# Moving a table copy behind the last adjacency chunk, and two short tiles behind that chunk's lists

## The chip, the core and the metric

The kernel runs on one core of one Trainium2 chip. The metric is the device time of one execution in microseconds (us). Three runs of the kernel before gave 941.17, 937.54 and 940.53 us, so the median is 940.53 us. A separate execution was recorded by the hardware profiler; the durations below come from that one.

## What is computed

The reference is a two-layer graph network on 3327 nodes with 512 features and one sparse adjacency matrix (each node also neighbours itself). Cut to what matters:

```python
# layer 0: graph attention, 4 heads of 128
feats  = einsum('nf,hfo->hno', x, W)
logits = leaky_relu(e_s[:, :, None] + e_n[:, None, :], 0.2) - 1e10 * (1 - A)
out0   = relu(einsum('hnm,hmo->hno', softmax(logits), feats) + b)   # heads side by side
x      = layernorm(x + out0)
# layer 1: gated sum of an attention and a plain neighbour sum
attn_a = sigmoid(concat([adj @ x, x]) @ Wa.T + ba)                  # attn_b likewise
e      = where(adj != 0, exp(-leaky_relu(s_left[:, None] + s_right[None, :], 0.01)), 0)
x_a    = (e / (sum(e) + 1e-5)) @ (x @ W_sa)
x_b    = adj @ (x @ W_gcnb) + b_gcnb
x      = layernorm(x + sigmoid(attn_a * x_a + attn_b * x_b))
```

## The kernel before

All of it is `sparse_pass`; a dense pass stands behind it for graphs that are too dense, and does not run here. Nodes are padded to 3328, that is 26 tiles of 128. The first 12 tiles form group 0, the other 14 form group 1. In each group the nodes are sorted by their number of neighbours, so that each tile has a fixed cap of neighbours (`CAPS`, line 26).

**First stage, lists and features.** The adjacency comes in seven column chunks of 512 (the last has 256). Each chunk is 13 loads of two row tiles (`load_adj`, line 218) into 12 buffers (`AT`, line 34), all issued by SyncE (SP) in program order. For every chunk, TensorE (PE) sums the ones into codes (`add_codes`, line 396), ScalarE (ACT) takes them out of PSUM (`take_codes`, line 413), PE transposes them (`turn_codes`, line 421), and VectorE (DVE) picks the neighbours of each node from them (`top_codes`, `decode`, `pick`). Alongside, `features` (line 365) computes one tile of projected features, and GpSimd (POOL) writes the rows to `table0` in HBM. When a group's chunks are done its lists are sorted by length (`rank_a`, `rank_b`; for group 0 also `sort0`). The lists of group 0 are complete before the last chunk comes; the ranks of group 1 need the last chunk.

**`table0`.** For each node of group 0 it has two rows side by side (`twos`): the node's own x, and its features. The x rows are copied from HBM to HBM by one DMA, `x_rows` (line 238), which SP issues before the 13 loads of the last chunk. For group 1 a second table, `own1`, is put together by two more copies (lines 989 and 990), which are the next DMAs on SP.

**Gathers.** Neighbours' rows are fetched by indirect DMAs, one for each list position of a tile (128 rows of 2080 bytes), all issued by POOL in order (`indirect`, line 615). A tile's first gather brings the pair of own x and own features. They go to a ring of 42 slots (`RING`, line 33). `plan` (line 620) lists every gather of a layer in `waiting`; `gather` (line 656) issues them as long as the ring has room; `free` gives a tile's slots back. `at_first` (line 874) takes the gathers of features of the first two tiles out of the list and issues them ahead of the two own pairs, since these alone need the copied x rows.

**Second stage, layer 0.** Tiles are taken in `order0` (line 735): first tiles 11 and 10 (caps 5 and 6, called `early`), then tile 0 (cap 14, with an extra row for nodes over the cap), tile 1, and so on. For each tile `weigh_a` and `weigh_b` (DVE, with an exponential on ACT) make the attention weights, `attend` (line 784) scales each gathered row (DVE, every third one ACT) and sums the rows on PE with an identity matrix in fp32, and `finish` (line 881) adds the result to own x. The two early tiles are handled inside the first stage: they are weighed before `add_codes` of the last chunk, attended right after it, and finished before its `turn_codes`. From tile 0 on, a loop over the 26 tiles (line 948) does the rest, followed by layer 1 (lines 1139 to 1199), which gathers from `table1`.

Each engine takes its instructions in program order; the order above is written by hand. The part of the last chunk reads:

Of the kernel before, what the change touches and what calls it, by code (L numbers as in the profile page):

```python
# [25 lines left out]
CAPS = (14, 12, 11, 10, 9, 9, 8, 8, 7, 6, 6, 5) + (14, 13, 11, 10, 10, 9, 9, 8, 8, 7, 7, 6, 5, 4)  # L26
# [6 lines left out]
RING = 42  # L33
# [45 lines left out]
def sparse_pass(  # L79
# [39 lines left out]
    nc = tc.nc  # L119
# [8 lines left out]
    chunks = list(range(0, NP, CH))  # L128
    T0 = (0, NG[0])
# [7 lines left out]
    N0 = NG[0] * P  # L137
    table0 = dram.tile([N0 + NP, ROW], F32, name="table0")
    twos, singles = table0[: 2 * N0, :], table0[2 * N0 :, :]
# [36 lines left out]
    def place(j):  # L176

        return (0, j) if j < NG[0] else (1, j - NG[0])
# [5 lines left out]
    def row1(j):  # L184
        g, i = place(j)
        return x1[g][:, i, :]

    def slots(j):

        return S + 1 if j in T0 else CAPS[j] + 1  # L190
# [18 lines left out]
    def load_x(i):  # L209
        if i < len(chunks):  # L210
            cw = min(CH, NP - chunks[i])
            xc = xcs[i] = pj.tile([P, KT, CH], F32, tag="xc", name=f"xc{i}", bufs=3)
            nc.sync.dma_start(xc[:, :, :cw], xB[i] if cw == CH else xL)
# [20 lines left out]
        asa_rows.append(a_row)  # L234
    load_x(1)
    for i in range(len(chunks)):
        if i == len(chunks) - 1:
            x_rows = nc.sync.dma_start(twos.rearrange("(n t) w -> n t w", t=2)[:, 0, :], xo[:N0]).ins
            tc.add_to_no_dep_group("x rows", x_rows)
        load_adj(i)  # L240
        load_x(i + 2)


    nc.vector.memset(ones, 1.0)
# [368 lines left out]
    waiting, ends_at = [], {}  # L613

    def indirect(out_, table, ap):
        return nc.gpsimd.indirect_dma_start(  # L616
            out=out_, out_offset=None, in_=table, in_offset=bass.IndirectOffsetOnAxis(ap=ap, axis=0)
        ).ins
# [37 lines left out]
    def gather():  # L656

        while waiting and waiting[0][0] - freed[0] <= RING:
            indirect(*waiting.pop(0)[1:])

    def free(j):

        freed[0] = ends_at[j]
# [71 lines left out]
    order0 = first[-2:][::-1] + first[:-2] + second[-3:-2]  # L735
# [8 lines left out]
    def weigh_a(j):  # L744
        c = slots(j)
        g, i = place(j)
        w = ws[j] = m0.tile([P, S + 1, H], F32, tag="w", name=f"w{j}", bufs=3)
        es = srt[g][:, i : i + 1, S + 2 : S + 2 + H].bitcast(F32)
        for s0, n, buf, o in got[j]:
            nc.vector.tensor_add(w[:, s0 : s0 + n, :], buf[:, o : o + n, F : F + H], es.to_broadcast([P, n, H]))  # L750
        if j in T0:
            logit = m0.tile([P, H], F32, tag="logit", name=f"logit{j}")
            nc.vector.tensor_add(logit, stair[j][:, F : F + H], es2[g])
            small = psx.tile([P, B * H], F32, tag="pcol", name=f"to_nodes{j}", bufs=2)
            nc.vector.tensor_tensor(
                w[:, C0 + 1 :, :], to_nodes(m0, small, f"n{j}", logit),
                no_step.rearrange("p (b o) -> p b o", o=1).to_broadcast([P, B, H]), ALU.add,
            )
        nc.vector.scalar_tensor_tensor(w[:, :c], w[:, :c], 0.2, w[:, :c], ALU.mult, ALU.max)
        mx = m0.tile([P, 1, H], F32, tag="mx", name=f"mx{j}")  # L760
        nc.vector.tensor_reduce(mx[:, 0, :], w[:, :c].rearrange("p s h -> p h s"), AX.X, ALU.max)
        nc.vector.tensor_sub(w[:, :c], w[:, :c], mx.to_broadcast([P, c, H]))  # L762
        nc.scalar.activation(w[:, :c], w[:, :c], AF.Exp)  # L763

        for s0, n, buf, o in got[j]:
            a = max(s0, 1)
            if a == s0 + n:
                continue
            nc.scalar.copy(srt[g][:, i, a : s0 + n], buf[:, o + a - s0 : o + n, F + H])
        if j in T0:  # L770
            nc.scalar.copy(ids2[g], stair[j][:, F + H : F + H + 1])
        nc.scalar.copy(row1(j)[:, 0:F], got[j][0][2][:, 0, 0:F])

    def weigh_b(j):
        c, w = slots(j), ws[j]
        den = m0.tile([P, 1, H], F32, tag="den", name=f"den{j}")
        nc.vector.tensor_reduce(den[:, 0, :], w[:, :c].rearrange("p s h -> p h s"), AX.X, ALU.add)
        nc.vector.reciprocal(den, den)
        nc.vector.tensor_mul(w[:, :c], w[:, :c], den.to_broadcast([P, c, H]))  # L779
        if j in T0:  # L780
            small = psx.tile([P, B * H], F32, tag="pcol", name=f"to_rows{j}", bufs=2)
            ws2[j] = to_rows(m0, small, f"n{j}", w[:, C0 + 1 :, :])

    def attend(j, lean, between):


        w = ws[j]
        acc = accs[j] = ps.tile([P, F], F32, tag="acc", name=f"acc{j}", bufs=2)
        if not lean:
            nc.tensor.matmul(acc, ident, bias0, start=True, stop=False)  # L790
        for s0, n, buf, o in got[j]:
            for s in range(s0, s0 + n):
                gv = buf[:, o + s - s0, 0:F].rearrange("p (h o) -> p h o", h=H)
                if s % 3 == 2:
                    for h in range(H):
                        nc.scalar.activation(gv[:, h, :], gv[:, h, :], AF.Copy, scale=w[:, s, h : h + 1])  # L796
                else:
                    nc.vector.tensor_tensor(  # L798
                        gv, gv, w[:, s, :].rearrange("p (h o) -> p h o", o=1).to_broadcast([P, H, FO]), ALU.mult
                    )  # L800
                row = buf[:, o + s - s0, 0:F]
                if lean and s == 0:
                    nc.vector.tensor_add(row, row, bias0)
                nc.tensor.matmul(  # L804
                    acc, ident, row, start=(lean and s == 0), stop=(s == CAPS[j] and j not in T0)
                )
                if s == 2:
                    between()
        if j in T0:
            gv = stair[j][:, 0:F].rearrange("p (h o) -> p h o", h=H)  # L810
            nc.vector.tensor_tensor(
                gv, gv, ws2[j].rearrange("p (h o) -> p h o", o=1).to_broadcast([P, H, FO]), ALU.mult
            )
            nc.tensor.matmul(acc, to_node, stair[j][:, 0:F], start=False, stop=True)
# [54 lines left out]
        ps = ctx.enter_context(tc.tile_pool(name="ps", bufs=1, space=PSUM))  # L869
        ring = gp.tile([P, RING, ROW], F32, name="ring")  # L870

    early = order0[:2]

    def at_first():

        a, b = (CAPS[j] + 1 for j in early)
        waiting[: a + b] = waiting[1:a] + waiting[a + 1 : a + b] + [waiting[0], waiting[a]]
        for _ in range(a + b - 2):
            tc.declare_no_dep(indirect(*waiting.pop(0)[1:]), group="x rows", reason="they read rows of features only")

    def finish(j):
        y = row1(j)[:, 0:F]
        nc.vector.scalar_tensor_tensor(y, accs[j], 0.0, y, ALU.max, ALU.add)
        free(j)
        gather()
# [5 lines left out]
    for i in range(len(chunks)):  # L891
        if i == len(chunks) - 1:
            open_pools()
            for j in order0:
                plan(table0, j)
            at_first()
            gather()
            for j in early:
                weigh_a(j)
                weigh_b(j)  # L900
        add_codes(i)
        if i == len(chunks) - 1:
            for j in early:
                attend(j, False, lambda: None)
        take_codes(i)
        if i == len(chunks) - 1:
            for j in early:
                finish(j)
        more(1)
        if i == NC0:  # L910
            rankis[0] = rank_b(0)
            sort0(rankis[0])
        turn_codes(i)
        if i == NC0 + 2:
            climb(0, p0, psl.tile([P, CH], F32, tag="pc1", name="climb0")[:, : B + H])
        top_codes(i)
        decode(i)
        pick(i)
        if i == NC0 - 1:
            rank_a(0)  # L920
        if i == NC0:
            with nc.allow_non_contiguous_dma(reason="a word of a row"):
                nc.scalar.dma_start(
                    twos.rearrange("(t p o) w -> p t o w", p=P, o=2)[:, :, 1, F + H : F + H + 1],
                    ranks[0][:, : NG[0]].rearrange("p (t w) -> p t w", w=1),
                )
        more(4)
        if i == 0:
            stairs_ready()
# [12 lines left out]
        nc.tensor.matmul(psum, ones, v1[:, k, :], start=(k == 0), stop=(k == KT - 1))  # L942
    nc.vector.tensor_copy(v1sum, psum)
    norm = Norm(m0, "n0", {3, 7, 11, 15, 19, 22, 24, 25})
    weigh_a(order0[2])
    weigh_b(order0[2])
    ready = [[], []]
    for i in range(NT + 3):
        for args in ready[0]:
# [9 lines left out]
        if 0 < i <= NT:  # L959
            j = order0[i - 1]  # L960
# [189 lines left out]
    for i in range(NT + 3):  # L1150
        j, j1, jp, jpp = at_(i), at_(i + 1), at_(i - 1), at_(i - 2)
# [500 lines left out]
```

## Time and profile before

| | us |
|---|---|
| median of 3 runs | 940.53 |
| span of the profiled execution | 1066.8 |
| time of that run | 1068.62 |
| busy PE, DVE, POOL, ACT in that span | 814.2, 735.3, 593.5, 289.0 |
| start to first row scaled for tile 0 on DVE | 270.8 |
| from there to the last row written to `table1` | 359 |
| from there to the end | 437 |

The profiled execution is 126 us longer than the median of the others, so its durations are somewhat long for an ordinary run. Busy shares are averages over stages with different limits. In the first 250 us the DMA engines are busy all the time; after that they are at 56 to 63 per cent. The granted TensorE clock was 0.865 of full speed on average; it falls to one half when PE has had little to do.

The page's table of DMA issues gives the sizes that matter here: 13 loads of 256 KB for the last chunk, 3120 KB for the copy of x rows, and 3640 KB for each of the two copies to `own1`.

### The profile page before, as it was taken

Reading aid. Unit: us, or ns where it says so; the run is one execution under the profiler, and the core shown is the slowest. Engines: PE = TensorE matmul, PEld = TensorE weight load, DVE = VectorE, ACT = ScalarE, POOL = GpSimd, SP = SyncE. Lnnn points to the kernel's source line nnn. Section 1 sums busy time; section 2 is a strip of 40 time slices with the busy share of each in tenths; the row PEclk is TensorE's granted clock in tenths of the full one; section 3 lists DMA queues with packets and bytes.
Section 4 is the critical chain, followed back from the end, with each engine's and each line's share of the span. In section 5 each row is a group of like instructions: output and inputs, shape, how many; then the busy total and the mean of one; then the engine's idle time right before and its main releaser. Section 6 shows DMA issues by size and latency. Waiting matters only on the chain. (4 is left out here: it accounts for less than half of the span.)

```text
span 1066.8 us, 10313 instructions
## 1 busy us (share of the span) xinstructions
PE 814.2 (76%) x2518; PEld 426.4 (40%) x2518; DVE 735.3 (69%) x2100; ACT 289.0 (27%) x820; POOL 593.5 (56%) x641
## 2 busy tenths in 40 slices
PE   5698972521987877777987956639999999969993
PEld 4476751201443433333443422214444444434441
DVE  3486788407857467655756757348798998989973
ACT  1122220200424243432434422112323123232331
POOL 7511243760566666465766247765667777757611
PEclk9898995565898879788987977769999999989997
DMA  9999899991477668586676127755656666746400
GB/s 341 371 361 399 342 325 351 377 386 53 126 212 235 199 192 251 144 307 197 183 210 198 61 98 196 207 164 140 188 144 186 183 182 182 195 129 182 167 28 35
DMA packets 73349, 224.68 MB, mean 211 GB/s; under 512 B 12736, under 2 KB 16784, under 8 KB 72384
## 3 DMA queue, kind: packets, MB, share of 16 engines
q0 software_dynamic: 46368, 153.69, 48.8%
q1 hardware_dynamic: 24256, 68.13, 16.8%
q10 hardware_dynamic: 2656, 2.10, 0.6%
q8 instruction: 23, 0.38, 0.1%
q14 instruction: 46, 0.38, 0.1%
HBM read 203.02 MB, written 31.51 MB: 220 GB/s over the span
## 5 line engine op out<-in xcount | busy, mean ns | idle before, releaser
L616 POOL DMA_INDIRECT ring<-table,srt x464 | 475.2, 1024 | 265.1 <-issue 98.8
L804 PE MATMUL acc<-ring,ident 128*128 128x512 f32 x504 | 261.9, 667 | 56.6 <-ACT ring L796 18.5
L1097 DVE SCALAR_TENSOR_TENSOR sw<-ring,e,sw 128x512 f32<-128x512 f32 x226 | 169.4, 750 | 11.6 <-ACT sw L1081 4.7
L804 PEld LDWEIGHTS acc<-ring,ident 128*128 128x128 f32 x504 | 101.7, 212 | 178.8 <-issue 109.2
L1118 PE MATMUL acc<-ring,ident 128*128 128x512 f32 x264 | 126.4, 613 | 13.8 <-DMA ring<-table,srt 9.7
L372 PE MATMUL pf<-w,xc 128*128 128x260 f32 x416 | 105.3, 417 | 13.1 <-DVE w L312 13.1
L798 DVE TENSOR_TENSOR ring<-ring,w 128x512 f32<-128x512 f32 x176 | 111.3, 691 | 1.7 <-DVE w L779 1.2
L1137 PE MATMUL po<-wsa,sT 128*128 128x512 f32 x208 | 98.4, 617 | 18.5 <-ACT sT L1130 10.3
L372 PEld LDWEIGHTS pf<-w,xc 128*128 128x128 f32 x416 | 85.8, 209 | 30.1 <-DVE w L312 13.8
L1137 PE MATMUL po<-wg,sT 128*128 128x512 f32 x208 | 93.8, 593 | 0.8 <-issue 0.8
L796 ACT ACTIVATE ring<-ring,w 128x128 f32<-128x128 f32 x304 | 91.5, 389 | 0.0
L1118 PEld LDWEIGHTS acc<-ring,ident 128*128 128x128 f32 x264 | 50.7, 194 | 81.8 <-issue 54.7
L1137 PEld LDWEIGHTS po<-wsa,sT 128*128 128x128 f32 x208 | 40.9, 199 | 73.4 <-issue 59.3
L1099 DVE TENSOR_TENSOR ring<-ring 128x512 f32<-128x512 f32 x94 | 65.0, 692 | 3.2
L403 PE MATMUL pc<-at,pow 128*32 128x512 bf16 (+1 forms) x182 | 24.6, 414 | 53.0 <-DMA at<-in_adjB 24.4
L384 POOL DMA_DIRECT2D table<-row x26 | 14.3, 549 | 87.2 <-ACT st L381 84.6
L763 ACT ACTIVATE w<-w 128x40 f32<-128x40 f32 (+10 forms) x26 | 6.2, 237 | 201.5 <-DVE w L762 124.8
L1137 PEld LDWEIGHTS po<-wg,sT 128*128 128x128 f32 x208 | 39.3, 190 | 49.9 <-issue 49.7
L1130 ACT COPY sT<-pt 128x512 f32<-128x512 f32 x52 | 28.7, 587 | 102.0 <-remote 48.8
L376 ACT COPY row<-pf 128x512 f32<-128x512 f32 x26 | 15.2, 585 | 96.2 <-PE pf L372 50.6
L829 ACT COPY xt<-x1t 128x512 f32<-128x512 f32 x26 | 15.2, 584 | 94.9 <-remote 39.2
L835 PEld LDWEIGHTS pcol<-v,xt 128*128 128x128 f32 x208 | 33.1, 228 | 17.3 <-issue 14.1
(254 smaller groups left out, 941.7 us busy)
## 6 DMA issues: line engine op xcount, KB each, us to landing
at<-in_adjB SPq DMA_DIRECT2D x78, 512.0 KB
ring<-table,srt POOLq DMA_INDIRECT x464
table<-row POOLq DMA_DIRECT2D x26, 260.0 KB
xc<-in_xB SPq DMA_DIRECT2D x6, 1024.0 KB
own<-in_xo SPq DMA_DIRECT2D x1, 3640.0 KB
own<-table SPq DMA_DIRECT2D x1, 3640.0 KB
at<-in_adjL SPq DMA_DIRECT2D x13, 256.0 KB
table<-in_xo SPq DMA_DIRECT2D x1, 3120.0 KB
```

The lines of the kernel that those rows point to most:

```text
L372: nc.tensor.matmul(pf[:, hh, :HC], xc[:, k, o : o + P], w0[:, k, hh, :], start=(k == 0), stop=(k == KT - 1))
L403: nc.tensor.matmul(pc[32 * c : 32 * c + 32, : nt * P], pow2[:, s, :], loaded[i, m], start=(s == 0), stop=(m + 1 not in ms or s == 3),)
L616: return nc.gpsimd.indirect_dma_start(out=out_, out_offset=None, in_=table, in_offset=bass.IndirectOffsetOnAxis(ap=ap, axis=0)).ins
L796: nc.scalar.activation(gv[:, h, :], gv[:, h, :], AF.Copy, scale=w[:, s, h : h + 1])
L798: nc.vector.tensor_tensor(gv, gv, w[:, s, :].rearrange("p (h o) -> p h o", o=1).to_broadcast([P, H, FO]), ALU.mult)
L804: nc.tensor.matmul(acc, ident, row, start=(lean and s == 0), stop=(s == CAPS[j] and j not in T0))
L835: nc.tensor.matmul(pcol, xt1[:, k, :], v1[:, k, :], start=(k == 0), stop=(k == KT - 1))
L1097: nc.vector.scalar_tensor_tensor(sw, g[:, i, 0:F], e[:, s : s + 1], sw, ALU.mult, ALU.add)
L1099: nc.vector.tensor_add(g[:, i, 0:F], g[:, i - 1, 0:F], g[:, i, 0:F])
L1118: nc.tensor.matmul(plain[j], to, row, start=(not sums_of_two and i == 0), stop=(sums_of_two and i == len(rows) - 1),)
L1130: nc.scalar.copy(sT, pt)
L1137: nc.tensor.matmul(proj[j], sT[:, k, :], wt[:, k, :], start=(half + k == 0), stop=(half + k == KT))
```

## The change

The copy of x rows is issued after all loads of the last chunk, and so just ahead of the copies to `own1`. `at_first` now covers three tiles: it issues the 26 gathers of features of tiles 11, 10 and 0 (5 + 1, 6 + 1 and 14 + 1 list positions and the extra row, less the three own pairs), and leaves the three own pairs at the head of what waits. The weighing, attending and finishing of tiles 11 and 10 move from around `add_codes` of the last chunk to behind the ranks of group 1; tile 0 is weighed between their `attend` and their `finish`.

```diff
     for i in range(len(chunks)):
-        if i == len(chunks) - 1:
-            x_rows = nc.sync.dma_start(twos.rearrange("(n t) w -> n t w", t=2)[:, 0, :], xo[:N0]).ins
-            tc.add_to_no_dep_group("x rows", x_rows)
         load_adj(i)
         load_x(i + 2)
+    x_rows = nc.sync.dma_start(twos.rearrange("(n t) w -> n t w", t=2)[:, 0, :], xo[:N0]).ins
+    tc.add_to_no_dep_group("x rows", x_rows)
...
-    early = order0[:2]
-
     def at_first():
 
-        a, b = (CAPS[j] + 1 for j in early)
-        waiting[: a + b] = waiting[1:a] + waiting[a + 1 : a + b] + [waiting[0], waiting[a]]
-        for _ in range(a + b - 2):
-            tc.declare_no_dep(indirect(*waiting.pop(0)[1:]), group="x rows", reason="they read rows of features only")
+        whole, part, owns = [], [], []
+        for j in order0[:3]:
+            n = CAPS[j] + 1 + (j in T0)
+            whole, part, owns = whole + waiting[:n], part + waiting[1:n], owns + waiting[:1]
+            del waiting[:n]
+        assert whole[-1][0] <= RING
+        waiting[:0] = owns
+        for args in part:
+            tc.declare_no_dep(indirect(*args[1:]), group="x rows", reason="they read rows of features only")
...
             at_first()
             gather()
-            for j in early:
-                weigh_a(j)
-                weigh_b(j)
         add_codes(i)
-        if i == len(chunks) - 1:
-            for j in early:
-                attend(j, False, lambda: None)
         take_codes(i)
-        if i == len(chunks) - 1:
-            for j in early:
-                finish(j)
         more(1)
...
     norm = Norm(m0, "n0", {3, 7, 11, 15, 19, 22, 24, 25})
+    for j in order0[:2]:
+        weigh_a(j)
+        weigh_b(j)
+    for j in order0[:2]:
+        attend(j, False, lambda: None)
     weigh_a(order0[2])
     weigh_b(order0[2])
+    for j in order0[:2]:
+        finish(j)
     ready = [[], []]
```

## The prediction

> **What bounds the kernel now.** First the windows: busy time by engine over the stretch in which the first stage ends (columns: stretch, its us, PE, PEld, DVE, ACT and POOL busy with counts, granted TensorE clock, DMA share, GB/s).
>
> ```profile
> 164.00:178.00 14.00, 4.36 (x16) 2.29 (x16) 12.19 (x55) 0.68 (x1) 10.45 (x11) 0.50 1.03 324
> 178.00:187.00 9.00, 0.40 (x2) 0.11 (x2) 8.14 (x39) 0.00 (x0) 0.44 (x1) 0.50 1.02 360
> ...
> 191.00:204.00 13.00, 3.42 (x17) 1.30 (x15) 8.77 (x26) 6.92 (x23) 9.95 (x11) 0.50 1.04 395
> 204.00:222.00 18.00, 15.37 (x34) 6.57 (x32) 0.00 (x0) 0.47 (x1) 13.25 (x14) 0.88 1.03 387
> 222.00:244.00 22.00, 0.00 (x0) 0.00 (x0) 1.40 (x3) 0.00 (x0) 12.29 (x13) 0.50 0.98 368
> 244.00:264.00 20.00, 4.52 (x12) 2.96 (x12) 16.54 (x70) 0.00 (x0) 0.00 (x0) 0.50 0.04 15
> 264.00:271.00 7.00, 3.01 (x9) 2.15 (x10) 4.89 (x18) 3.05 (x10) 0.95 (x1) 0.50 0.15 39
> ```
>
> Up to 244 the DMA engines are full; up to 191 DVE is nearly full too. From 204 to 244 DVE does 1.4 us of work in 40, and POOL then has none for 20. The whole chip waits for a chain, which the timelines give. SP first (start, duration):
>
> ```profile
> 156.87 0.56 SPq L238 DMA_DIRECT2D table<-in_xo  x1
> 157.52 32.45 SPq L222 DMA_DIRECT2D at<-in_adjL  x13
> 190.02 0.67 SPq L989 DMA_DIRECT2D own<-in_xo  x1
> ```
>
> The copy of x rows goes out at 156.9, all 13 loads of the last chunk after it. POOL:
>
> ```profile
> 164.35 1.00 POOL L616 DMA_INDIRECT ring<-table,srt  x1 [6.48 <-DMA at<-in_adjB]
> ...
> 186.56 0.94 POOL L616 DMA_INDIRECT ring<-table,srt  x1 [8.72 <-DMA table<-in_xo]
> ...
> 267.61 0.95 POOL L616 DMA_INDIRECT ring<-table,srt  x1 [24.72 <-ACT x1a L772]
> ```
>
> Eleven gathers of features start at 164.35, one each 1.25 us; the own pairs wait until 186.56 for the copy; at 267.61 POOL comes out of 24.7 us of idleness, because the ring is full of rows that tile 0 has yet to use. DVE:
>
> ```profile
> 193.89 0.18 DVE L750 TENSOR_TENSOR w<-ring,srt 128x24 f32<-128x24 f32 x1 [2.24 <-DMA at<-in_adjL]
> ...
> 197.49 5.63 DVE L798 TENSOR_TENSOR ring<-ring,w 128x512 f32<-128x512 f32 x9
> 229.22 0.69 DVE L883 SCALAR_TENSOR_TENSOR x1a<-acc,x1a 128x512 f32<-128x512 f32 x1 [26.09 <-remote]
> 240.57 0.69 DVE L883 SCALAR_TENSOR_TENSOR x1a<-acc,x1a 128x512 f32<-128x512 f32 x1 [10.66 <-remote]
> 243.98 0.40 DVE L71 MAX8 ent<-pv 128x8 f32<-128x224 f32 x1 [2.72 <-remote]
> ...
> 263.76 0.22 DVE L750 TENSOR_TENSOR w<-ring,srt 128x60 f32<-128x60 f32 x1 [0.23 <-issue]
> ...
> 270.81 0.68 DVE L798 TENSOR_TENSOR ring<-ring,w 128x512 f32<-128x512 f32 x1
> ```
>
> The early tiles are weighed at 193.9 and scaled by 203.1. Then DVE waits for PE: their sums come at 229.2 and 240.6, the lists of the last chunk only at 244.0, and tile 0 is weighed at 263.8 and attended from 270.8. PE:
>
> ```profile
> 203.24 2.07 PE L790 MATMUL acc<-bias,ident 128*128 128x512 f32 x2
> ...
> 212.65 6.17 PE L804 MATMUL acc<-ring,ident 128*128 128x512 f32 x14
> 218.66 0.47 PE L427 MATMUL pv<-ident,v 128*128 128x128 f32 x3
> ```
>
> PE's last adjacency matmul starts at 202.9; then come 15 fp32 matmuls for the early tiles (two of bias, 6 + 7 of rows, each recorded as two) and the transposes that the lists wait for. The records have them done by 218.7, but DVE and POOL see the results some 22 us later (DVE sees the transposes at 243.98, recorded from 218.66 to 221.64). The view names only "remote" for it; the cause is open, and I carry both values.
>
> So the path to tile 0 is: last chunk landed (203), early tiles on PE, lists on DVE, weighing. Two things sit ahead of the lists that they don't need: the copy, and the early tiles.
>
> **What the Trainium skill says.** "DMA: Bandwidth & Descriptors", section "Queues, rings and completion order": descriptors of one ring are consumed in order, and each DMA engine takes turns between queues by packets. The trace fits: the last chunk lands only after the copy ahead of it on SP's queue, while gathers run beside both. The same page, section "Anatomy of one DMA": DMA engines don't wait on semaphores, the issuing sequencer does; so the own pairs hold POOL (8.7 us before 186.56). "TensorE: Matmul & The Clock Gate", section "The HAM clock gate": an idle PE falls to half clock and needs sustained work to come back; here 0.50 from 222 to 271, and 1.00 in the slice from 275 to 300.
>
> **The change part by part.**
>
> *The copy moves behind 13 loads on SP; the copies to `own1` are still behind it.* The last load of the chunk before is in use at 165.3. Before, the copy of 3.19 MB then took until 186.6, 21.2 us (150 GB/s beside gathers), and the chunk of 3.41 MB until 202.9, 16.3 us (209 GB/s). After, the chunk comes first: 165.3 + 16.3 = 181.6 at that rate. But 26 gathers now run beside it, not 11: 26 x 1.25 = 32.5 us, 164.4 to 196.9, at 266 KB each 213 GB/s; of the 358 GB/s of the stage (150 to 200) 145 are left, and 3.41 MB take 23.5 us, to 188.8. I take 188.8. Taking, transposing and signalling cost up to 4 us (the transposes show 3.4 between 240.57 and 243.98): lists from 193. DVE is done with the lists of the chunk before at 191.6, so landing earlier gains only 1.4 us more. The copy ends between 181.6 + 21.2 = 203 and 188.8 + 21.2 = 210.
>
> *26 gathers ahead of own pairs.* Fifteen gathers issue earlier instead of after the pairs: same number, no cost on POOL, since its ring is full long before tile 0. The three pairs then go at 203 to 210. Between the first pair's issue (186.56) and its weighing (193.89) lie 7.3 us: early tiles ready at 210 to 217.
>
> *Lists ahead of the early tiles.* DVE needs 263.5 - 244.0 = 19.5 us for lists and ranks, which now run from 193 to 212.5, beside the copy. This hides the late own rows up to 212.5; later arrival counts one for one. I take 215 for the start of the early tiles, between 212.5 and 217.
>
> *The early tiles behind the lists.* Both weighings 3.7 us (193.89 to 197.57), first scaled row 0.7, the 15 matmuls 15.6 as recorded (203.24 to 218.8); the other scaling (5.6 us on DVE, 4.8 on ACT) hides beside them. Tile 0's small matmul for its extra row queues on PE behind these 15, and DVE behind it; from there to attending tile 0 is 6.5 us (264.34 to 270.81), and two finishes add 1.4. Sum: 215 + 3.7 + 0.7 + 15.6 + 6.5 + 1.4 = 242.9.
>
> *Before, on the same terms.* With PE's results at their recorded times: transposes done 221.6, lists 19.5 to 241.1, then 7.3 to tile 0 (263.5 to 270.8): 248.4. So the gain is 248.4 - 242.9 = 5.5 us, between 3.2 (pairs at 217.3) and 8.0 (212.5). It is small because PE's 15 matmuls stay on the path: the chunk is 14 us earlier, but two weighings and two finishes join the chain and the own rows become late. With the lag of 22.4 us as seen before and gone after, it is 27.9; with the lag in both, 5.5 again.
>
> *After tile 0.* Nothing there is tied to absolute time: the ring is full at its start in both, the `own1` copies are done by about 245 (the DMA share falls to 0.04 after 244) and needed first at 372. The 360 us of layer 0 and 437 us of layer 1 shift whole.
>
> Against the profiled execution: span 1066.8 - 5.5 = 1061. It is 126 us longer than the median, so the lag may well belong to that execution; on the median I take 5.5 unscaled: 940.5 - 5.5 = 935.0.
>
> **The rivals.**
>
> *The lag is real in ordinary runs and goes away.* For it: DVE and POOL both saw it. Against: PE's matmuls move to 220 to 237, still under the `own1` copies, where it was seen. Between 16 and 28 us gained; with 22: 918.
>
> *Nothing to see.* The gathers' packets crowd the loads so that the chunk lands near 200: lists 204.5 to 224, early tiles then, tile 0 at 224 + 27.9 = 251.9, 3.5 later than 248.4: 944, within what can be told. For it: full DMA engines; against: POOL's issue caps gathers at 213 GB/s.
>
> *Own rows decide (slower).* The copy now shares the DMA engines with the backlog of 26 gathers, and its pairs with the first `own1` copy behind it. Tile 0 starts at C + 7.3 + 27.9, with C the landing of the copy; equal to before at C = 213.2, measurably slower from 218. With the chunk at 145 GB/s and the copy at the same 145 (22 us), C is 211; if the pairs need 10 us more beside the `own1` copies, tile 0 starts at 256.2: 7.8 slower, 948. For it: 150 GB/s is what the copy got with 11 gathers beside it. Against: POOL stops at 197, and the copy then runs alone.
>
> **How the numbers follow.** A measurement of this kernel can tell about 0.5% (4.7 us) from no change. Forecast 0.50 (gain 0.5 to 10: of it 0.29 beyond 4.7 us, 0.19 within, 0.02 lost to slower); lag gone 0.20, all faster; nothing 0.10; own rows 0.20, nearly all slower. Faster 0.49, same 0.29, slower 0.22. The likeliest case alone gives 931 to 940; the range takes in the middle of the lag case and most of the slow one: 918 to 948.
>
> **What would show it.** SP: 13 loads, then the copy, then `own1`. PE's last adjacency matmul near 189 (wrong if over 197). DVE at the last lists from about 193 without a gap to 212 (the step on lists). 26 gathers to 197, then a wait of POOL until 203 to 210; DVE's first weighing at 212 to 217: if it waits for the own pair beyond 218, the own rows decide. Tile 0's first scaled row near 243 in an undisturbed record, and up to 265 with the lag. POOL's idleness of 24.7 us before 267.61 should shrink by what tile 0 gains. What would make me wrong most easily is the lag: it is four times the forecast gain.

## The result, and the profile after

The changed kernel took 930.73 us (median of 5 runs, 927.72 to 933.13) against 937.85 us for the kernel before (median of 5, 937.32 to 941.17). The ratio is 0.9922, with a 95% interval of 0.9897 to 0.9947: about 7 us faster (7.1 by the medians), between 5 and 10. The same pair timed again (after_again, where 0.992 and a first row of tile 0 at 239 were expected) gave 0.9925 (0.9898 to 0.9952), 7.5 us by the medians.

One thing has to be known first. Later runs met two kinds of chip: on one the median of the kernel before is about 937 us, on the other 1068 to 1079 us. ("Kind" means no more than this; it may be a condition of the chip at that time.) The profiled execution shown so far (1068.62 us) fits the second kind; the record of the changed kernel below is of the first (span 931.1 us, from the first instruction to the last). The right partner for it is a second record of the kernel before on a chip of the first kind ("before, second record" below, span 932.7 us). Differences between kernels are taken within one kind.

The windows of the changed kernel, in the columns used before (stretch, its us, PE, PEld, DVE, ACT and POOL busy with counts, TensorE clock, DMA share, GB/s):

```profile
191.00:204.00 13.00, 0.00 (x0) 0.00 (x0) 11.76 (x58) 0.00 (x0) 3.16 (x5) 0.50 1.02 363
204.00:222.00 18.00, 11.30 (x20) 5.56 (x21) 13.30 (x38) 6.50 (x22) 13.17 (x14) 0.50 1.02 377
222.00:244.00 22.00, 17.24 (x39) 8.06 (x38) 10.74 (x28) 7.24 (x25) 17.34 (x14) 0.82 0.88 345
244.00:264.00 20.00, 20.00 (x63) 10.16 (x62) 14.42 (x35) 6.62 (x22) 15.73 (x15) 1.00 0.65 181
```

Between 191 and 222 DVE is now at work for 25.1 of 31 us; in the second record of the kernel before it was 13.7, and 0.8 of the 12 us from 204 to 216. The chunk's lists run there while the DMA engines (still full, 1.02) bring own rows. After 247 POOL no longer pauses.

The SyncE timeline of the changed kernel shows the copy behind the 13 loads, and the `own1` copy behind it:

```profile
155.57 19.50 SPq L222 DMA_DIRECT2D at<-in_adjL  x13
175.13 1.31 SPq L239 DMA_DIRECT2D table<-in_xo  x1
176.49 11.41 SPq L989 DMA_DIRECT2D own<-in_xo  x1
```

POOL: 26 gathers from 162.4, then 8.9 us of waiting for the copy; later one gather is recorded as 8 us long instead of 0.95. Counted along the ring, the gather behind it is the first that needs a slot from which PE must first take a row of tile 0:

```profile
162.41 1.00 POOL L615 DMA_INDIRECT ring<-table,srt  x1 [6.12 <-DMA at<-in_adjB]
...
203.74 0.94 POOL L615 DMA_INDIRECT ring<-table,srt  x1 [8.92 <-DMA table<-in_xo]
...
238.78 7.98 POOL L615 DMA_INDIRECT ring<-table,srt  x1 [0.30 <-issue]
```

DVE of the changed kernel, its timeline (start, duration, instruction, idle time before it and what ended it). Weighing of tile 11 begins at 212.66, after DVE has waited 1.5 us for own rows; the early tiles' rows are scaled from 216.38, DVE then waits 10 us for tile 0's small matmul behind the early tiles' sums, and tile 0's rows begin at 239.23:

```profile
212.66 0.18 DVE L749 TENSOR_TENSOR w<-ring,srt 128x24 f32<-128x24 f32 x1 [1.48 <-DMA ring<-table,srt]
...
216.38 5.50 DVE L797 TENSOR_TENSOR ring<-ring,w 128x512 f32<-128x512 f32 x9
...
232.49 0.20 DVE L754 TENSOR_TENSOR w<-to_nodes,no_step 128x40 f32<-128x40 f32 x1 [10.12 <-PE to_nodes L673]
...
235.72 1.28 DVE L885 SCALAR_TENSOR_TENSOR x1a<-acc,x1a 128x512 f32<-128x512 f32 x2
...
239.23 6.11 DVE L797 TENSOR_TENSOR ring<-ring,w 128x512 f32<-128x512 f32 x10
```

The PE timeline of the same record, where the early tiles' matmuls stand ahead of tile 0's small one:

```profile
186.20 0.40 PE L402 MATMUL pc<-at,pow 128*32 128x256 bf16 x2 [0.90 <-DVE key L71]
...
210.44 2.06 PE L789 MATMUL acc<-bias,ident 128*128 128x512 f32 x2
217.12 8.32 PE L803 MATMUL acc<-ring,ident 128*128 128x512 f32 x12 [4.62 <-DVE ring L797]
...
226.13 6.17 PE L803 MATMUL acc<-ring,ident 128*128 128x512 f32 x14
232.14 0.31 PE L673 MATMUL to_nodes<-spread_n,to_node 128*128 128x40 f32 x2
```

PE's last adjacency matmul is at 186.20 (200.9 in the second record of the kernel before). Of the 15 matmuls of the early tiles, the first bias runs at 210.44, and the other 14 from 217.12 to 232.3.

The same stage in the second record of the kernel before, first PE with the rows of the early tiles, then DVE's timeline:

```profile
203.05 5.91 PE L804 MATMUL acc<-ring,ident 128*128 128x512 f32 x12
209.66 6.17 PE L804 MATMUL acc<-ring,ident 128*128 128x512 f32 x14
```

```profile
209.00 0.69 DVE L883 SCALAR_TENSOR_TENSOR x1a<-acc,x1a 128x512 f32<-128x512 f32 x1 [9.25 <-PE acc L804]
215.94 0.69 DVE L883 SCALAR_TENSOR_TENSOR x1a<-acc,x1a 128x512 f32<-128x512 f32 x1 [6.25 <-PE acc L804]
216.54 0.39 DVE L71 MAX8 ent<-pv 128x8 f32<-128x224 f32 x1
...
243.62 6.11 DVE L798 TENSOR_TENSOR ring<-ring,w 128x512 f32<-128x512 f32 x10
```

And POOL's timeline in that record:

```profile
240.41 0.94 POOL L616 DMA_INDIRECT ring<-table,srt  x1 [6.65 <-ACT x1a L772]
249.44 1.71 POOL L616 DMA_INDIRECT ring<-table,srt  x1 [8.08 <-PE acc L804]
```

No lag here: the sums of the early tiles come at 209.0 and 215.9, the lists begin at once, and tile 0 starts at 243.6, not 270.8. POOL stops twice, 6.65 and 8.08 us, since the ring is full of tile 0's rows: it waits for the copy of tile 0's own x (ACT) and for its first row on PE. The twelve records of tile 11's rows show a price of the new order: 5.91 us here, at a granted clock of 0.90 (203 to 209), and 8.32 us in the changed kernel, at 0.64 (217 to 225.3), after the lists, during which PE has little to do (clock 0.50 from 191 to 217).

### The profile page after: what moved, and what is told of

It is laid out like the page before. It is cut to its first block, busy times and chain, and to the rows that moved or that the text cites. A ratio compares the mean times of both kernels' runs of the same rounds, so it can differ in the third digit from the quotient of the medians.

```text
span 931.1 us, 10307 instructions
## 1 busy us (share of the span) xinstructions
PE 785.4 (84%) x2518; PEld 413.5 (44%) x2518; DVE 735.7 (79%) x2100; ACT 288.2 (31%) x820; POOL 601.9 (65%) x641
## 5 line engine op out<-in xcount | busy, mean ns | idle before, releaser
L615 POOL DMA_INDIRECT ring<-table,srt x464 | 483.1, 1041 | 159.6 <-issue 60.3
L803 PE MATMUL acc<-ring,ident 128*128 128x512 f32 x504 | 240.8, 622 | 20.6 <-DVE ring L802 13.3
L803 PEld LDWEIGHTS acc<-ring,ident 128*128 128x128 f32 x504 | 95.3, 198 | 133.4 <-issue 74.6
L1118 PE MATMUL acc<-ring,ident 128*128 128x512 f32 x264 | 126.5, 608 | 19.6 <-DVE ring L1099 10.2
L1137 PE MATMUL po<-wsa,sT 128*128 128x512 f32 x208 | 95.0, 600 | 0.3 <-ACT sT L1130 0.3
L1118 PEld LDWEIGHTS acc<-ring,ident 128*128 128x128 f32 x264 | 49.8, 193 | 90.0 <-issue 44.5
L1169 ACT ACTIVATE za<-za 128x512 f32<-128x512 f32 x26 | 16.4, 632 | 152.9 <-DVE za L1167 152.9
L1130 ACT COPY sT<-pt 128x512 f32<-128x512 f32 x52 | 28.4, 587 | 37.8 <-PE pt L1128 37.8
L834 PEld LDWEIGHTS pcol<-v,xt 128*128 128x128 f32 x208 | 28.1, 197 | 14.1 <-issue 11.4
(254 smaller groups left out, 940.5 us busy)
```

The lines of the kernel that those rows point to most:

```text
L615: return nc.gpsimd.indirect_dma_start(out=out_, out_offset=None, in_=table, in_offset=bass.IndirectOffsetOnAxis(ap=ap, axis=0)).ins
L803: nc.tensor.matmul(acc, ident, row, start=(lean and s == 0), stop=(s == CAPS[j] and j not in T0))
L834: nc.tensor.matmul(pcol, xt1[:, k, :], v1[:, k, :], start=(k == 0), stop=(k == KT - 1))
L1118: nc.tensor.matmul(plain[j], to, row, start=(not sums_of_two and i == 0), stop=(sums_of_two and i == len(rows) - 1),)
L1130: nc.scalar.copy(sT, pt)
L1137: nc.tensor.matmul(proj[j], sT[:, k, :], wt[:, k, :], start=(half + k == 0), stop=(half + k == KT))
```

## The experiments

Times of the stage, read from each record (us from the start of the span). Each is the start of an instruction; the ranks count by the last of theirs. The first five rows are from chips where the median of the kernel before is about 937 us, the others from chips where it is 1068 to 1079 or fit these.

| record | last adjacency matmul | first own pair on POOL | early tiles weighed | group 1 ranks done | tile 0's first row | POOL's 60th gather |
|---|---|---|---|---|---|---|
| before, second record (before_b) | 200.9 | 182.6 | 189.7 | 236.1 | 243.6 | 258.6 |
| changed (after) | 186.2 | 203.7 | 212.7 | 210.9 | 239.2 | 255.1 |
| changed (after_again) | 184.0 | 202.1 | 211.3 | 210.2 | 237.5 | 253.2 |
| own_later | 183.7 | 212.7 | 219.7 | 211.2 | 245.1 | 261.3 |
| in_loop | 181.2 | 198.1 | 211.9 | 211.2 | 234.0 | 245.0 |
| before, first record | 202.9 | 186.6 | 193.9 | 263.3 | 270.8 | 285.7 |
| before_again | 204.5 | 186.7 | 194.2 | 252.8 | 260.3 | 275.1 |
| copy_only, copy_only_b | 182.8, 182.7 | 193.2, 193.2 | 202.2, 202.3 | 261.3, 259.7 | 268.8, 267.2 | 283.9, 282.2 |
| lists_only, lists_only_b | 202.3, 203.5 | 184.9, 186.3 | 235.8, 236.0 | 235.1, 235.3 | 262.0, 261.8 | 276.5, 278.0 |
| eleven, eleven_b | 180.6, 181.2 | 191.7, 191.8 | 214.1, 213.4 | 213.4, 212.7 | 246.0, 245.4 | 264.7, 264.1 |
| pool_extra | 185.5 | 203.7 | 229.5 | 228.8 | 254.7 | 270.9 |

### Was the lag the kernel's or the execution's? (before_again, before_b)

No edit. What was expected:

> The kernel before, unchanged, for a second record. If the lag between PE's recorded ends and what DVE and POOL saw (22 us around 220 to 244) belonged to that one execution: a span near 938 us, the last lists start within 4 us of PE's last transposes, and tile 0's first scaled row lies at 248 (245 to 252). If the lag is a property of the order of work (the rival): again near 270, whatever the span.

> The kernel before once more, for a record on this call's chip. On a chip of the 938 kind: tile 0's first scaled row at 248 (245 to 252) and no lag of PE's results. On one of the 1079 kind: 260 to 271, with the lag.

The first landed on a chip of the slower kind: 1093.86 us, tile 0 at 260.3. The second gave 934.85 us and tile 0 at 243.6, with no lag. So the lag between PE and its readers (22 us in the first record; in before_again DVE takes the two sums some 13 and 8 us after PE's recorded ends) belonged to that kind of chip, not to the order of work. The list of waits says where such time sits; here the longest of it in before_again (engine and line, what ended the wait, us in total, times, longest):

```profile
ACT sT L1130 <- remote: 80.6, 12, 21.8
```

In before_b and the other four records of the faster kind no wait ends on "remote". On that kind of chip PE, DVE and ACT all stand still at times for a cause that the record does not name; what it is stays open.

### The copy alone (copy_only, copy_only_b)

```diff
     for i in range(len(chunks)):
-        if i == len(chunks) - 1:
-            x_rows = ...
         load_adj(i)
         load_x(i + 2)
+    x_rows = ...
```

> The kernel before with the copy of x rows alone moved behind the 13 loads; 11 gathers, early tiles still ahead of the lists. Theory (a chain of landing, lists and early tiles): the chunk lands near 182 to 186, but weighing the early tiles waits for own rows (copy near 203, weighing near 210) and the lists wait behind them: tile 0 near 260 instead of 248, about 11 us slower than before, 949. Rival (the gain comes from the chunk landing sooner): as fast as the changed kernel, near 931.

> The copy alone behind the 13 loads. Theory: early tiles wait for own rows and hold back the lists behind them: early tiles weighed near 202, tile 0 at 250 to 258 against 243.6 before, 60th gather 7 to 15 us later than before's 259, total 944 to 952. Rival (the chunk's earlier landing is the gain): 931 or less. On a chip of the other kind the ratio was 1.020.

Both met the slower kind of chip. The ratios to before were 1.0202 (1.0141 to 1.0263) and 1.0018 (0.9949 to 1.0087): the two intervals do not meet, so on such chips the total does not tell this apart. The stage shows more, alike on both chips. DVE and PE in copy_only:

```profile
202.25 0.18 DVE L749 TENSOR_TENSOR w<-ring,srt 128x24 f32<-128x24 f32 x1 [8.59 <-DMA ring<-table,srt]
...
205.86 5.64 DVE L797 TENSOR_TENSOR ring<-ring,w 128x512 f32<-128x512 f32 x9
215.07 0.69 DVE L882 SCALAR_TENSOR_TENSOR x1a<-acc,x1a 128x512 f32<-128x512 f32 x1 [3.58 <-PE acc L803]
222.22 0.69 DVE L882 SCALAR_TENSOR_TENSOR x1a<-acc,x1a 128x512 f32<-128x512 f32 x1 [6.45 <-PE acc L803]
227.78 0.40 DVE L71 MAX8 ent<-pv 128x8 f32<-128x224 f32 x1 [4.88 <-remote]
```

```profile
182.77 0.40 PE L402 MATMUL pc<-at,pow 128*32 128x256 bf16 x2 [0.32 <-DMA at<-in_adjL]
...
206.64 8.39 PE L803 MATMUL acc<-ring,ident 128*128 128x512 f32 x12 [21.47 <-DVE ring L797]
...
221.74 0.56 PE L426 MATMUL pv<-ident,v 128*128 128x128 f32 x4
```

The chunk is there 22 us sooner than in before_again (182.8 against 204.5), yet DVE sits idle 8.6 us until own rows come, weighs the early tiles 8 us later than before, and reaches the chunk's lists only at 227.8, behind the early tiles' sums. PE waits 21.5 us for the early tiles' rows, and turns the chunk's codes 39 us after its last adjacency matmul: landing sooner is not used. Tile 0 starts at 268.8 and 267.2; the two records of the kernel before on such chips have 260.3 and 270.8, so no gain shows. How large the loss would be is not measured: lists and ranks take 33.5 and 37.8 us in these two records, 23.2 in before_again and 19.5 in before_b. With 19.5, and the 7.5 us from there to tile 0 of before_b, tile 0 would start at 249 to 255, an estimate, against 243.6; no run of this kernel on the faster kind shows it.

### The order alone (lists_only, lists_only_b)

The changed kernel with the copy put back and `order0[:2]` in `at_first`:

```diff
     for i in range(len(chunks)):
+        if i == len(chunks) - 1:
+            x_rows = ...
         load_adj(i)
         load_x(i + 2)
-    x_rows = ...
...
-        for j in order0[:3]:
+        for j in order0[:2]:
```

> The changed kernel with the copy back ahead of the 13 loads and 11 gathers ahead of own rows: only the early tiles behind the lists. Theory: the chunk lands near 203, lists 206 to 225.5, then 28 us as in the changed kernel: tile 0 near 253.6, 5 us slower than before, 943. Rival (the order of lists and early tiles alone brings the gain): near 931.

> Only the early tiles behind the lists, copy ahead of the chunk, 11 gathers. Theory: lists start near 204 and end near 223.5, early tiles follow, tile 0 at 250 against 243.6: total 940 to 945, slower than before by 3 to 8. Rival (the order alone is the gain): 931 or less. On a chip of the other kind the ratio was 0.987, which fits the rival there.

Ratios 0.9873 (0.9803 to 0.9942) and 1.0061 (0.9971 to 1.0150), again from the slower kind and again not in agreement. The first rests on 3 of 22 runs; the medians of all runs are above before on both chips (1084.7 to 1079.0, 1080.7 to 1067.9). In the stage the chunk lands at 202.3, the ranks are done at 235.1 (before_again: 252.8), the early tiles come behind them, and tile 0 starts at 262.0 and 261.8, between the two records of before (260.3 and 270.8). Lists and ranks took 28.6 and 30.0 us here; with 19.5 tile 0 would start at 251 to 253, an estimate, against 243.6 in before_b. So no gain shows, and whether the expected loss of 5 us is right stays open.

### Eleven gathers instead of 26 (eleven, eleven_b)

```diff
-        for j in order0[:3]:
+        for j in order0[:2]:
             n = CAPS[j] + 1 + (j in T0)
```

> The changed kernel with 11 instead of 26 gathers ahead of own rows. Theory (the ring has a lead, so 15 gathers sooner or later cost nothing): 931, between 928 and 935, with tile 0 near 239. Rival (POOL's gathers bound what follows, so the 26 bring the gain): 15 x 1.25 = 19 us of gathers come later, most of the gain is lost, 936 or more, and tile 0 or tile 1 waits for its rows.

> The changed kernel with 11 gathers ahead of own rows, on a chip of the 938 kind if there is one. Theory as predicted (26 or 11 make no difference): 928 to 934, ratio to before near 0.992. Second theory, formed on the last call (total time follows the moment of POOL's 60th gather, 253 in the changed kernel, 259 in the one before): the copy lands about 10 us sooner with fewer gathers beside it, own pairs near 192, so the 60th gather comes at 252 to 257: 929 to 934 as well, for another reason. Rival (the 26 bring the gain): 15 x 1.25 = 19 us lost on POOL, 60th gather beyond 260, 937 or more.

Slower kind of chip both times: 0.9831 (0.9687 to 0.9975) and 0.9970 (0.9908 to 1.0032), with no timing of the changed kernel, with its 26, on the same chip. Whether the 26 add to the total is therefore open. (pool_extra below is the changed kernel up to its loop and ran on the chip of eleven_b. It has tile 0 at 254.7 against 245.4, but in it DVE's lists of the chunk before end at 209.2 instead of 193.0, behind waits of up to 3 us such as come and go on that kind of chip, so it doesn't settle this.) What the records do show is the trade: with 11 gathers beside them the chunk and the copy land sooner, and own pairs go at 191.7 and 191.8 instead of 202 to 204 with 26; the fifteen gathers then come behind the pairs. The lists start no sooner (193.8 and 192.9), since DVE is at those of the chunk before until then. These two are also the kernels with both other parts of the change, and their tile 0 starts at 246.0 and 245.4, 14 us before that of before_again, 16 us before lists_only and 21 to 23 before copy_only. So the two parts, of which neither showed a gain singly, give one together. Part of these differences is lag: lists and ranks took 19.6 and 19.8 us here, 28.6 to 37.8 in the four records of the single parts.

### Own rows later (own_later)

```diff
-        waiting[:0] = owns
+        waiting[9:9] = owns
```

> The changed kernel with the three own pairs issued nine gathers later (behind tile 1's own pair and eight of its rows, which wait for the copy as well): 9 x 1.25 = 11.3 us. Theory: own rows and lists arrive together, so lateness counts one for one: the early tiles are weighed at 222 to 224 instead of 212.7, tile 0 starts 10 us later, total 9 to 11 us above the changed kernel, slower than before. Rival (own rows have slack behind the lists): within 3 us of the changed kernel.

On a chip of the faster kind: 938.04 us against 929.29 for the changed kernel on the same chip; ratio to before 1.0005 (0.9989 to 1.0021). DVE in own_later:

```profile
219.65 0.18 DVE L749 TENSOR_TENSOR w<-ring,srt 128x24 f32<-128x24 f32 x1 [8.25 <-DMA ring<-table,srt]
...
223.31 5.50 DVE L797 TENSOR_TENSOR ring<-ring,w 128x512 f32<-128x512 f32 x9
...
245.07 5.50 DVE L797 TENSOR_TENSOR ring<-ring,w 128x512 f32<-128x512 f32 x9
```

The early tiles are weighed at 219.7 instead of 211.3, tile 0 starts 7.6 us later and the total is 8.7 us longer, each somewhat less than expected, as it took 7.0 us from the first pair to the weighing instead of 9.2. Own rows have no slack behind the lists: their lateness counts nearly one for one, and about 8 us of it eat the whole gain.

### The early tiles as turns of the loop (in_loop)

```diff
-    for j in order0[:2]:
-        weigh_a(j)
-        weigh_b(j)
-    for j in order0[:2]:
-        attend(j, False, lambda: None)
-    weigh_a(order0[2])
-    weigh_b(order0[2])
-    for j in order0[:2]:
-        finish(j)
+    weigh_a(order0[0])
+    weigh_b(order0[0])
...
-        if 2 <= i < NT:
+        if i < NT:
             attend(order0[i], i >= 3, lambda: third is None or columns2(third))
...
-            if i > 2:
-                finish(j)
+            finish(j)
...
-        if 2 <= i < NT - 1:
+        if i < NT - 1:
             weigh_a(order0[i + 1])
```

> The changed kernel with tiles 11 and 10 taken as the first two turns of the loop instead of ahead of it. Theory: the 10 us in which DVE waits for tile 0's small matmul behind both tiles' 15 matmuls shrink, as tile 11's turn overlaps tile 10's: tile 0's first row 2 to 5 us sooner, total 1 to 4 us below the changed kernel, at the edge of what can be told. Rival (two tiles ahead of the loop are worth their place): slower than the changed kernel.

On the same chip: 920.72 us (918.25 to 924.71), ratio to before 0.9836 (0.9808 to 0.9863). It beats the changed kernel by 8.6 us and the one before by 16.1. DVE in in_loop:

```profile
213.66 2.50 DVE L797 TENSOR_TENSOR ring<-ring,w 128x512 f32<-128x512 f32 x4
...
217.91 3.20 DVE L797 TENSOR_TENSOR ring<-ring,w 128x512 f32<-128x512 f32 x5
221.82 0.69 DVE L885 SCALAR_TENSOR_TENSOR x1a<-acc,x1a 128x512 f32<-128x512 f32 x1 [0.71 <-PE acc L803]
...
230.68 0.20 DVE L754 TENSOR_TENSOR w<-to_nodes,no_step 128x40 f32<-128x40 f32 x1 [5.29 <-PE to_nodes L673]
...
234.00 6.10 DVE L797 TENSOR_TENSOR ring<-ring,w 128x512 f32<-128x512 f32 x10
```

Tile 11's sum is taken at 221.8 (changed kernel: 233.9 in after_again), so its ring slots are free that much sooner, and DVE's wait for tile 0's small matmul falls from 9.6 to 5.3 us. Tile 0 starts 3.5 us sooner on DVE, as forecast; but the total falls by 8.6, where 1 to 4 were expected. The PE and POOL timelines say why. First after_again:

```profile
241.31 2.74 PE L803 MATMUL acc<-ring,ident 128*128 128x512 f32 x6
```

```profile
237.90 7.08 POOL L615 DMA_INDIRECT ring<-table,srt  x1 [0.30 <-issue]
245.28 1.33 POOL L615 DMA_INDIRECT ring<-table,srt  x1 [0.30 <-issue]
```

And in_loop at the same place:

```profile
234.74 2.84 PE L803 MATMUL acc<-ring,ident 128*128 128x512 f32 x6 [0.22 <-DVE ring L797]
```

```profile
234.07 1.43 POOL L615 DMA_INDIRECT ring<-table,srt  x1 [0.30 <-issue]
...
239.60 1.32 POOL L615 DMA_INDIRECT ring<-table,srt  x1 [0.50 <-PE acc L803]
```

PE starts tile 0's rows 6.6 us sooner. In after_again the transposes and sorting matmuls that follow the early tiles (234.7 to 240.0) stand ahead of them; in in_loop those of tile 11 run at 228.5 to 230.5, and those of tile 10 behind tile 0's rows. POOL's 54th gather, which needs the first slot that PE must empty of tile 0, goes at 245.28 in after_again, behind one recorded as 7.08 us long, and at 236.13 in in_loop, where none near there takes over 1.5. POOL's 60th gather comes 8.2 us sooner, and that is what the total follows. (Own pairs left 4 us sooner in this record, at 198.1, which the edit doesn't touch; how much of POOL's lead that gave is not separated.)

### POOL lengthened (pool_extra)

```diff
+        if i == 9:
+            for _ in range(28):
+                nc.gpsimd.memset(columns, 0.0)
```

> The changed kernel with 28 small writes of a dead tile on POOL at the loop's turn 9 (about 6 to 8 us of POOL work near 350 us, nothing else). Theory (from the 60th gather on POOL's gathers are back to back, so layer 0 moves with POOL): the last row of layer 0 and the total come 5 to 8 us later, 935 to 938. Rival (PE or DVE set the pace and the ring has a lead of some gathers): no more than 2 us later.

It met the slower kind of chip: ratio to before 1.0060 (0.9995 to 1.0124), without the changed kernel beside it. POOL spent 7.3 us on the writes:

```profile
378.35 0.95 POOL L615 DMA_INDIRECT ring<-table,srt  x1 [0.30 <-issue]
379.30 7.29 POOL L983 MEMSET columns<- 128x128 f32 x28
387.09 0.95 POOL L615 DMA_INDIRECT ring<-table,srt  x1 [0.50 <-issue]
```

There POOL is not back to back anyway: 17 other steps of the 194 after the 60th gather are over 2.5 us, up to 5.7, where the records of the faster kind have none. The question was put to the wrong kind of chip, and the run leaves it open.

## Why the prediction was right, point by point

The forecast was 5.5 us (935.0 from 940.5); measured are 7.1 and 7.5 us, and 930.73 lies in the range (918 to 948), at the lower edge of what the likeliest case was to give (931 to 940). Of the 4.3 us between 935.0 and 930.73, 2.7 are the starting point (937.85 after two more runs). The sign was right, and so was the mechanism up to tile 0: the lists run while own rows come.

- **The copy behind 13 loads.** Forecast for the chunk: between 181.6 and 188.8, taken at 188.8; measured 186.2 and 184.0. Lists forecast from 193, done 212.5; measured from 191.3 and done at 211.1 (190.7 and 210.3 in after_again). What they waited for was DVE's lists of the chunk before (done 191.4 and 190.8), not the chunk, whose transposes were done some 3 to 5 us earlier. The copy was expected between 203 and 210; own pairs left POOL at 203.7 and 202.1, at the early end.
- **Own rows.** Early tiles were expected at 212.5 to 217, taken 215; measured 212.7 and 211.3. This is the term of the sum that was mis-sized most, by 2 to 4 us. The copy took 17.5 and 18.1 us from the chunk's last matmul to the first pair (21.2 charged, after 188.8); from there to the weighing it took 8.9 and 9.2 (7.3 charged). The price per us of lateness was right, as own_later showed.
- **The early tiles behind the lists.** 15 matmuls: forecast 15.6, measured 15.2 for 14 of them, as the first bias had run ahead and tile 11's rows took 8.3 us (7.6 in the record that the forecast used); from tile 0's small matmul to its first row 6.5 + 1.4 = 7.9, measured 7.1. Tile 0 was forecast at 242.9 and came at 239.2 and 237.5.
- **Before, on the same terms.** 248.4 was worked out by taking the lag away; before_b has 243.6. So both sides were 4 to 5 us too late and the difference held: forecast 5.5, measured 243.6 - 237.5 = 6.1 (4.4 to the first record of the changed kernel). That the two errors are alike is luck. On the side of before it is all in where the lists begin (221.6 taken from the first record, 216.5 in before_b); on the other side it is mostly own rows.
- **What follows tile 0.** The prediction let layer 0 "shift whole". For this change that held: from tile 0's first row to the end it is 689.1 us in before_b, 691.9 and 690.3 in the changed kernel. The step that does not hold in general is the tie to tile 0: in_loop has 685.1. Counted from POOL's 60th gather, the five records of the faster kind (before_b, after, after_again, own_later, in_loop) have 674.1, 676.0, 674.6, 676.9 and 674.1 us. On these chips POOL's gathers are back to back from about there: 194 of them take 249 us in before_b and 250 in after_again, 1.28 us each, which is nearly POOL's own pace of 1.25. The full ring, which the prediction took as cover ("no cost on POOL, since its ring is full long before tile 0"), is then where POOL loses time: before_b stops it for 6.65 and 8.08 us. own_later moved the 60th gather by +8.1 us and the total by +8.7, in_loop by -8.2 and -8.6, while tile 0 moved by +7.6 and -3.5. That POOL's pace is the cause is inferred from this; the direct test did not land where it could be read.

Of the rivals, "the lag goes away" was about the chip of that record and not about the order of work: before_b has no lag to lose. "Nothing to see" needed the chunk near 200, and it came at 186. "Own rows decide" needed the copy beyond 213, and it came near 203.

That neither part brings tile 0 forward alone, and both together do, rests on stage times of records from the slower kind, with lag in them, and on the estimates above (249 to 255 and 251 to 253, against 243.6 before and 239.2 and 237.5 with both). Neither single part was run on the faster kind, and their totals are not settled.

## What to carry to other kernels

When work is moved out of the way of a chain, look for what the move makes late in its turn: here own rows became late by 20 us, and were free only because the lists took as long. Work that was put ahead of a loop to fill a hole should go back into the loop when the hole is gone; here that brought more than the change itself. And where one queue issues back to back for the rest of a stage, the moment from which it does so is what to move, not the start of the next tile.

## What was not expected of the hardware

The same kernel had a median of 937 us on one chip (25 runs, 933 to 941) and of 1079 and 1068 on two others (44 runs, 1053 to 1095, and 11 runs, 1056 to 1090). Up to the last adjacency matmul of the kernel before (200.9 and 204.5) the records of both kinds agree within 4 us. The rest comes after it, with many waits for which the record names no releaser, and POOL's 194 gathers after the 60th take 298 us in before_again instead of 249 in before_b. The waits are not only between engines. In pool_extra small DVE instructions wait some 1.2 us for the one before them on DVE; the starts of these two lie 1.41 us apart, and 0.25 in after_again:

```profile
189.73 0.21 DVE L442 TENSOR_SCALAR bn<-bn 128x96 int32<-128x96 int32 x1 [1.19 <-DVE bn L441]
191.14 0.26 DVE L444 TENSOR_TENSOR code<-ent,bn 128x96 f32<-128x96 f32 x1 [1.20 <-DVE bn L442]
```

A record of one kind next to a time of the other, as at the start of this case, shows a stall that the timed runs do not have.

The gather that is recorded as 7 to 8 us long ends within 0.01 us of the end of one DVE instruction, `BATCH_NORM_AGGREGATE` at line 693, in all three records that have it (after, after_again, own_later: 246.76 and 246.75, 244.98 and 244.98, 252.59 and 252.59). A run of DVE instructions with hardly a gap lies beside it each time; in in_loop the same gather beside such a run takes 1.43. What holds it is open.
